# Seven products for a graph layer's weight product, with the sums of the data on GpSimd

## The chip, the cores and the metric

The kernel runs on one core of one Trainium2 chip. The metric is the device time of one execution in microseconds, the median of several. Everything is float32.

The engines are named as the profile names them: PE is TensorE (PEld its loads of the stationary operand), DVE is VectorE, ACT is ScalarE, POOL is GpSimd, SP issues the DMA transfers.

## The reference, cut to what matters

The input `x` has 128 graphs of 64 nodes with 256 features. Four layers follow each other, each with a layer norm and a relu in front and a residual around it: two graph convolutions with LSTMs over windows of nodes, a graph convolution with batch norm, a graph layer with three weights, and causal attention inside each graph. The change concerns the third and touches the operands of the fourth:

```python
h = jnp.maximum(_layernorm(x, axis=-1), 0.0)
adj_0 = jnp.diag(jnp.diagonal(adj)); adj_1 = jnp.triu(adj, k=1); adj_2 = jnp.tril(adj, k=-1)
h = jnp.einsum('bjf,kfo->kbjo', h, W)                  # W: 3 x 256 x 256
out = jnp.einsum('ij,bjo->bio', adj_0, h[0]) + jnp.einsum('ij,bjo->bio', adj_1, h[1]) \
    + jnp.einsum('ij,bjo->bio', adj_2, h[2])
x = x + out + bias
```

## The kernel before, in words

The 8,192 tokens are cut into 16 blocks of 512. The first two layers, with the LSTMs and the two batch norms, take the first 1,460 us; the change leaves their code alone, but the sums of the new weights and the loads of those weights go into the last microseconds of the second layer. Everything else of the change is in the last stage, `rest`, which does layers 3 and 4 for one block.

For a block, `rest` loads the residual `x1` (L1198, a DMA on SP), applies the batch norm of the layer before to the features-by-tokens array (`affine`, L1205, VectorE), turns it to tokens by features on TensorE (`turn`, L1221) and adds `x1` on VectorE (`turned`, L1224). `norm` takes statistics on VectorE (L1235, L1236), the inverse root (`root`: an addition on VectorE, L1240, a power on GpSimd, L1241), the negative mean times that root (`shift`, L1244, VectorE), and normalizes with a relu on ScalarE (L1248). `biased` (L1261) adds the layer's bias to the residual on GpSimd.

`graphs3` (L1273) multiplies by the adjacency's three parts at once: for a half of the features and a half of the tokens, pairs of 64-row matmuls write two PSUM tiles, one copied to `ag` by ScalarE and one by VectorE (L1278). `weigh` (L1285) is the weight product: for each 128 tokens, six matmuls (two halves of the features times three weights) with a piece of `ag` stationary and 256 columns of `wl2` streaming, summed in PSUM. `weighed` (L1291) adds the result to the residual, 512 columns at a time, on VectorE.

Then comes layer 4: the norm again, `h3` turned (L1298) and copied (L1302), and the product with the queries' and keys' joint weights in seven-product form: `qsum` (L1313, VectorE) forms four sums of pieces of the data, `qproduct` (L1326) has seven products that accumulate into three PSUM tiles a, b and c, `qcopy` and `qadd` (L1330, L1333) take these out. `hv` (L1350, copied at L1354) gives the values, `scores` (L1360), `masked` (L1365), `largest` (L1370) and `exps` (L1373) the softmax, `turn_e` (L1381) and `turned_e` (L1385) its transpose, `attend` (L1391) the product with the values, `attended` (L1396, VectorE) adds it to the residual, and a DMA writes the block out (L1402).

The order on each engine is the order in which the program emits instructions. In `rest` every piece of work is put into a list with a label, `at(t, function, ...)`; the list is sorted by the labels and emitted. The labels look like microseconds but set the order alone. Blocks go in pairs, an even one E and an odd one O, with `PERIOD = 52.5` between the labels of two pairs. While a pair's weight products run, the next pair's blocks are turned and normalized (called N here). TensorE's order in a steady pair is: graphs of E and of O, E's products with the transposes of the preceding O's softmax and a turn of N among them, O's products with that O's attend and another turn of N, then E's query product and attention mixed with O's.

[...] `bank()` hands them out in a ring; `new_banks(psum=8)` makes one ring of eight, and a bank is given again only after the last reader of the tile that it held is done.

Of the kernel before, what the change touches and what calls it, by code (L numbers as in the profile page):

```python
# [9 lines left out]
F32 = mybir.dt.float32  # L10
AF = mybir.ActivationFunctionType
ALU = mybir.AluOpType
AX = mybir.AxisListType

P = 128
# [5 lines left out]
def kernel(ctx: ExitStack, tc: tile.TileContext, a: dict, out: bass.AP):  # L21
# [60 lines left out]
    def bank(pool="psum"):  # L82
        return banks[pool][1].tile([P, 512], F32, tag="ps", name="ps")
# [213 lines left out]
    OF = (None, A11, A12, S4, A22, S1, S2, S3)  # L297
# [50 lines left out]
    ROUND, HALF = 10.0, SUP // 2  # L348
# [288 lines left out]
    def at(t, fn, *args):  # L637
        events.append((t, len(events), fn, args))
# [154 lines left out]
    t = 0.0  # L793
    wt[0][0].append(wih0[0])
    for p in range(1, NL + 1):
# [8 lines left out]
        for k in range(0, len(pairs), 2):  # L804
            sts = [{"blk": blk, "N": blk[0][2] * GB, "p": p, "pool": pool}
                   for blk, pool in zip(pairs[k : k + 2], (lh0, lh1))]
            for j in range(p):
                for st in sts:
# [6 lines left out]
                    t = step(t, st, j, j == p - 1, l, wt[l], turn)  # L815
# [82 lines left out]
    with tc.tile_pool(name="pz", bufs=1, reuse_waits="tile") as pz:  # L898
# [13 lines left out]
        B = GATE * (NS - 2)  # L912
# [264 lines left out]

    PERIOD, HALF = 52.5, SUP // 2  # L1180
    NP = NS // 2
    with tc.tile_pool(name="pc", bufs=2, reuse_waits="tile") as pc, \
            tc.tile_pool(name="pc1", bufs=1, reuse_waits="tile") as pc1:
        events = []

        def rest(s, at, only_pair, t_T, t_n, t_G, t_W, t_h, t_QH, t_S, t_soft, t_E, t_O, end):
            first_, v = s == 0, {}
            y = [yslot(s, c) for c in range(KC)]

# [3 lines left out]
            def q2s(k):  # L1193
                return slice(2 * k, 2 * k + 2)
# [31 lines left out]
            def norm(src, tag, halves, t_rows, t_relu):  # L1226

                def new():
                    v["st"] = pc.tile([P, Q, 6], F32, tag="ln_st", name="ln_st", bufs=4)
                    v["mv"] = pc.tile([P, Q, 2], F32, tag="ln_mv", name="ln_mv", bufs=4)  # L1230
                    v["rn"] = pc.tile([P, 2, Q], F32, tag="ln_rn", name="ln_rn", bufs=4)
                    v[tag] = pc.tile([P, Q, D], F32, tag=tag, name=tag)

                def stats(q):
                    nc.vector.bn_stats(v["st"][:, q, :], v[src][:, q, :])  # L1235
                    nc.vector.bn_aggr(v["mv"][:, q, :], v["st"][:, q, :])  # L1236

                def root(qs):
                    rn = v["rn"][:, 0, qs]
                    nc.vector.tensor_scalar_add(rn, v["mv"][:, qs, 1], EPS)  # L1240
                    nc.gpsimd.tensor_tensor(rn, rn, mhalf[:, : qs.stop - qs.start], ALU.pow)  # L1241

                def shift(qs):
                    nc.vector.scalar_tensor_tensor(v["rn"][:, 1, qs], v["mv"][:, qs, 0], -1.0,  # L1244
                                                   v["rn"][:, 0, qs], op0=ALU.mult, op1=ALU.mult)

                def relu(q):
                    nc.scalar.activation(v[tag][:, q, :], v[src][:, q, :], AF.Relu,  # L1248
                                         bias=v["rn"][:, 1, q : q + 1], scale=v["rn"][:, 0, q : q + 1])

                at(t_rows[0] - 0.01, new)
                for q in range(Q):
                    at(t_rows[q // 2] + 0.6 * (q % 2), stats, q)
                for k, qs in enumerate((q2s(0), q2s(1)) if halves else (slice(0, Q),)):
                    at(t_relu[k] - 1.5, root, qs)
                    at(t_relu[k] - 0.1, shift, qs)
# [20 lines left out]
                    to = v["ag"][:, c, :, 2 * k * P : (2 * k + 2) * P]  # L1277
                    copy(to.rearrange("p k (q n) -> p q k n", q=2)[:, :, :, b * T : (b + 1) * T], half[b])  # L1278

            def weigh(k, q):  # L1280
                if q == 0:
                    v["W"] = two(bank())
                for n in range(3 * KC):
                    c, m = divmod(n, 3)
                    nc.tensor.matmul(v["W"][:, q, :], v["ag"][:, c, m, ts(2 * k + q, P)],  # L1285
                                     wl2[m][:, c, :], start=(n == 0), stop=(n == 3 * KC - 1))
# [32 lines left out]
            def qproduct(name, j):  # L1319
                new = ("q", name) not in v  # L1320
                if new:
                    v["q", name] = bank()[:, :HALF]
                if "qk" not in v:
                    v["qk"] = pc1.tile([P, KC, SUP], F32, tag="qk", name="qk")
# [9 lines left out]

            def qdirect(o):
                if o == 0:
                    v["qk"] = pc1.tile([P, KC, SUP], F32, tag="qk", name="qk")
# [65 lines left out]

            at(t_T - 8, load)
            for c in range(KC):
                at(t_T - (2 if first_ else 4.8 if s == 1 else 9) + (0.6 if s != 1 else 0.1) * c, affine, c)
            for k in range(2):
                if first_:
                    at(t_T - (2 - k) * 0.05, turn_chunk, k)
# [2 lines left out]
                at(t_T + 0.1 * k + 0.01, turned, k)  # L1412
            if first_:
                norm("x2", "h2", True, (t_T + 0.455, t_T + 1.8), (t_T + 3.2, t_T + 4.6))
                for q in range(Q):
                    at(t_T + 7 + 0.7 * q, biased, q)
            else:
                norm("x2", "h2", False, (t_n, t_n + 1.2), (t_n + (11.9 if s % 2 and s > 1 else 4.1),))
                for q in range(Q):
                    at(t_n + (18 if s % 2 else 10.5) + 0.7 * q, biased, q)  # L1420
# [47 lines left out]
        for i in range(NP):  # L1468
            t0, first_, end = PERIOD * i, i == 0, i == NP - 1

            def at(t, fn, *args, t0=t0):
                events.append((t0 + t, len(events), fn, args))

            rest(2 * i, at, i, -8.6 if first_ else -40.2, -38.3, 0, (7.0, 12.6), 29.0, 32.6, 40.0, 42.7,
                 46.3 if end else 48.46, 50.4 if end else 50.85, False)
            if first_:
                at(-7.6, weight_product, 2, wo, wvo)
                for k in range(8):
                    at(3.0 + 0.5 * k, qk_weights, k)
            rest(2 * i + 1, at, i, -3.0 if first_ else -27.6, 1.5 if first_ else -25.4, 12.3 if first_ else 3.5, (17.8, 26.5), 39.1,  # L1480
                 (42.0, 45.4, 48.7, 49.6, 52.1) if end else 42.0, 46.7 if end else 48.9,
                 49.5 if end else 59.5, 53.0 if end else 64.7, 53.8 if end else 75.6, end)
        for _, _, fn, args in sorted(events, key=lambda e: e[:2]):
            fn(*args)
    new_banks()
# [38 lines left out]
```

## Time and profile before

| what | us |
|---|---|
| median of 3 runs | 1876.81 (1876.74 to 1877.57) |
| profiled execution, its own time | 1876.78 |
| span of its instructions | 1875.1 |
| PE busy in the span | 1853.9 |
| DVE busy | 1129.4 |
| ACT busy | 925.7 |
| POOL busy | 645.4 |
| last stage, from the first pair's graphs (1461.46) to the end | 413.6 |

The span goes from the first to the last instruction of the profiled execution; 1.7 us of its own time lie around it. Busy time adds up the durations of an engine's instructions, with overlaps counted once. The clock granted to TensorE was 1.00 throughout. In the views, L with a number is a line of the kernel; a group's row gives what it writes and reads, the shapes, the number of instructions after x, then their busy time and the mean of one in ns. Each float32 matmul is two records of TensorE.

### The profile page before, as it was taken

What the parts mean: (1) busy time and instruction counts of PE and PEld (TensorE: products, weight loads), DVE (VectorE), ACT (ScalarE), POOL (GpSimd) and SP (SyncE); (2) the same over time, 40 slices, a digit from 0 to 9 for tenths busy, and PEclk for the clock granted to TensorE, in tenths of its full rate; (3) what the DMA queues carried; (4) which work ended last, traced back from release to release, by engine and by line L of the source; (5) the groups of instructions that cost most, each with busy time, mean ns of one, the idle gap of its engine ahead of it and who ended that gap; (6) DMA issues with size and microseconds to landing.
All of it is one profiled execution on the core that took longest, in us unless ns stands there. A gap on an engine that the chain in (4) does not pass through costs nothing.

```text
span 1875.1 us, 19841 instructions
## 1 busy us (share of the span) xinstructions
PE 1853.9 (99%) x7080; PEld 1168.8 (62%) x7080; DVE 1129.4 (60%) x2254; ACT 925.7 (49%) x1594; POOL 645.4 (34%) x553
## 2 busy tenths in 40 slices
PE   8999999999999999999999999999999999999999
PEld 7997444444445666666444444566444788888887
DVE  6775777634546435445633333588876776667674
ACT  6776666534435334433533333378685434433442
POOL 4451422443424433422442222267353412211220
PEclk9999999999999999999999999999999999999999
DMA  4110001000001000000000000243200111111101
GB/s 146 57 57 1 1 1 29 16 1 0 1 0 45 1 0 1 1 1 1 23 0 0 1 0 0 102 132 116 71 1 2 44 46 46 35 46 46 46 23 34
DMA packets 50642, 54.86 MB, mean 29 GB/s; under 512 B 3184, under 2 KB 45936, under 8 KB 50544
## 3 DMA queue, kind: packets, MB, share of 16 engines
q1 hardware_dynamic: 50096, 53.30, 8.9%
q8 instruction: 56, 0.92, 0.2%
q14 instruction: 42, 0.34, 0.1%
q10 hardware_dynamic: 448, 0.30, 0.0%
HBM read 36.55 MB, written 17.04 MB: 29 GB/s over the span
## 4 chain that ended last, share of the span: by engine, by line
PE 93%; DVE 3%; POOL 1%; ACT 1%; DMA 1%; issue 1%; SPq 0%; ACTq 0%; DVEq 0%; POOLq 0%
PE ps L686 34%; PE ps L692 19%; PE ps L1285 8%; PE ps L930 5%; PE ps L1047 4%; PE ps L1350 3%; PE ps L392 3%; PE ps L402 3%; PE ps L1326 2%; PE ps L431 2%; PE ps L1273 2%; PE ps L1360 2%; PE ps L1391 1%; PE ps L623 1%; PE ps L1298 1%; PE ps L579 1%
## 5 line engine op out<-in xcount | busy, mean ns | idle before, releaser
L708 DVE TENSOR_TENSOR gate<-gate,ps 128x512 f32<-128x512 f32 (+2 forms) x378 | 223.9, 620 | 449.0 <-PE ps L692 367.7
L686 PE MATMUL ps<-tx,wih 128*128 128x512 f32 (+2 forms) x996 | 441.2, 541 | 1.9 <-ACT gate L711 1.0
L686 PE MATMUL ps<-hT,wih 128*128 128x512 f32 (+2 forms) x756 | 338.5, 541 | 0.0
L711 ACT COPY gate<-ps 128x512 f32<-128x512 f32 (+2 forms) x252 | 134.5, 534 | 378.4 <-PE ps L692 325.4
L686 PEld LDWEIGHTS ps<-tx,wih 128*128 128x128 f32 x996 | 188.4, 190 | 188.2 <-issue 128.2
L704 ACT ACTIVATE gate<-gate,lbias 128x512 f32<-128x512 f32 (+2 forms) x252 | 216.7, 860 | 160.0 <-DVE gate L708 160.0
L692 PE MATMUL ps<-h,whh 128*128 128x512 f32 (+2 forms) x576 | 256.6, 527 | 0.0
L686 PEld LDWEIGHTS ps<-hT,wih 128*128 128x128 f32 x756 | 143.6, 190 | 141.6 <-issue 79.4
L692 PE MATMUL ps<-th,whh 128*128 128x512 f32 (+2 forms) x432 | 192.5, 527 | 0.0
L731 POOL TENSOR_TENSOR gate<-gate 128x1024 f32<-128x1024 f32 (+2 forms) x36 | 71.9, 2019 | 297.5 <-ACT gate L704 297.5
L1285 PE MATMUL ps<-wl,ag 128*128 128x256 f32 x768 | 172.1, 380 | 0.0
L692 PEld LDWEIGHTS ps<-h,whh 128*128 128x128 f32 x576 | 109.4, 190 | 100.2 <-issue 76.5
L1285 PEld LDWEIGHTS ps<-wl,ag 128*128 128x128 f32 x768 | 143.4, 190 | 20.2 <-ACT ag L1278 1.8
L731 POOL TENSOR_TENSOR cell<-gate 128x1024 f32<-128x1024 f32 (+2 forms) x36 | 79.4, 2225 | 174.8 <-ACT gate L704 174.8
L1241 POOL TENSOR_TENSOR ln_rn<-ln_rn,mhalf 128x4 f32<-128x4 f32 (+1 forms) x33 | 32.8, 995 | 300.8 <-DVE ln_rn L1240 300.3
L692 PEld LDWEIGHTS ps<-th,whh 128*128 128x128 f32 x432 | 82.1, 190 | 75.2 <-issue 57.4
L1248 ACT ACTIVATE h<-x,ln_rn 128x256 f32<-128x256 f32 x128 | 68.2, 593 | 103.3 <-DVE ln_rn L1244 103.3
L731 POOL TENSOR_TENSOR cell<-gate,cell 128x1024 f32<-128x1024 f32 (+2 forms) x31 | 62.8, 2044 | 110.2 <-ACT gate L704 110.2
L711 DVE COPY gate<-ps 128x512 f32<-128x512 f32 (+2 forms) x126 | 78.6, 624 | 20.8 <-PE ps L692 20.8
L704 ACT ACTIVATE gate<-ps,lbias 128x512 f32<-128x512 f32 (+2 forms) x126 | 79.6, 631 | 3.8 <-PE ps L692 1.0
L736 ACT ACTIVATE gate<-cell 128x1024 f32<-128x1024 f32 (+2 forms) x72 | 68.0, 951 | 26.1 <-POOL cell L731 26.1
L648 DVE TENSOR_TENSOR tx<-hT,tx 128x512 f32<-128x512 f32 (+2 forms) x70 | 57.7, 825 | 13.8 <-PE ps L686 10.2
(236 smaller groups left out, 2933.8 us busy)
## 6 DMA issues: line engine op xcount, KB each, us to landing
xt<-in_x_dram SPq DMA_DIRECT2D x30, 512.0 KB, 4.2
x1d<-xt SPq DMA_DIRECT2D x16, 512.0 KB, 3.0
x<-x1d SPq DMA_DIRECT2D x16, 512.0 KB, 4.9
out_dram<-x SPq DMA_DIRECT2D x15, 512.0 KB, 3.0
wih<-in_WihT_dram SPq DMA_DIRECT2D x16, 256.0 KB, 4.8
whh<-in_WhhT_dram SPq DMA_DIRECT2D x12, 256.0 KB, 4.8
xt<-in_x_dram SPq DMA_DIRECT2D x6, 128.0 KB, 3.2
wl<-in_W_dram SPq DMA_DIRECT2D x3, 256.0 KB, 3.6
```

The source lines that it names most:

```text
L648: yield nc.vector.tensor_sub(t[k], *((b[1][0], b[0][0]), (b[1][1], t[0]), (b[1][1], b[1][0]), (b[0][1], t[1 % len(t)]))[k])
L686: nc.tensor.matmul(wide(p_[:, :N]), wih[0][:, OF[k], gi, :], x_, start=first_, stop=(j == 0), skip_group_check=True)
L692: nc.tensor.matmul(p_[:, :N], whh[0][:, OF[k], gi, :], h_, start=False, stop=True, skip_group_check=True)
L704: nc.scalar.activation(to, r[bank_][:, :N] if bank_ else to, fn, bias=lbias[:, l, m : m + 1])
L708: nc.vector.tensor_add(slot(n, hc), slot(n, hc), r[bank_][:, :N])
L711: op(slot(n, hc), r[bank_][:, :N])
L731: fn(*((t["G"] if isinstance(t, dict) and "G" in t else st["c"])[:, n, :, : st["N"]] for t in tiles))
L736: nc.scalar.activation(o_, c, AF.Tanh)
L930: nc.tensor.matmul(r[name], con["w1"][:, OF[j], g, :], x_, start=new, stop=(name, j) in (("a", 4), ("b", 3), ("c", 2)), skip_group_check=True)
L1047: nc.tensor.matmul(banks[name], w2[:, OF[j], k, :], x_, start=(new and k == 0), stop=(k == 1), skip_group_check=True)
L1248: nc.scalar.activation(v[tag][:, q, :], v[src][:, q, :], AF.Relu, bias=v["rn"][:, 1, q : q + 1], scale=v["rn"][:, 0, q : q + 1])
L1285: nc.tensor.matmul(v["W"][:, q, :], v["ag"][:, c, m, ts(2 * k + q, P)], wl2[m][:, c, :], start=(n == 0), stop=(n == 3 * KC - 1))
```

## The change

The weight product of layer 3 gets the seven-product form that the query product has. `ag`, for each of the three adjacency parts, is cut in 2 x 2 (halves of features by halves of tokens), and so is each weight; four sums of the data (`gsum`, GpSimd, 768 columns each) and four sums of the weights (made once, `weight_sum`, GpSimd) feed seven products in place of eight. Pieces of data and their sums are stationary and 128 columns of weights stream (`gproduct`). The tiles a, b and c that the products accumulate into are taken out, as each partial sum is reached, by four evicts (`gevict`, residual plus tile) and three additions (`gadd`), each of 256 columns on VectorE. Block 0 uses the plain form, with 128 columns streaming too (`gdirect`).

Along with it: the banks become three for these accumulated tiles (`abc`) and a ring of five for all else; `qsum` goes from VectorE to GpSimd; `shift` becomes a multiplication on VectorE in `root` and one on GpSimd; the weights are one tile, loaded by four DMAs; `qk` and the data's sums use the space of weights that are no longer needed. The list is reordered: the next even block is turned at −14.5 where it was at −40.2, the next odd one at −43.5 where it was at −27.6, and the affines, roots, relus and biases that go with them, and O's later steps, get new labels.

```diff
-        wl2 = [weight(f"wl2_{k}", a["W"][k], late) for k in range(3)]
+        wl2 = late.tile([P, 7, 3, P], F32, tag="wl2", name="wl2")
+        for o in range(2):
+            for c in range(2):
+                nc.sync.dma_start(wl2[:, 2 * o + c], a["W"].rearrange(
+                    "m (c p) (o n) -> o c p m n", c=2, o=2)[o, c])
...
+        for k in range(4):
+            if k != 2:
+                at(B + 60 + 5.16 * k, weight_sum, wl2, k)
...
+    new_banks(abc=3, psum=5)
...
                 def root(qs):
-                    rn = v["rn"][:, 0, qs]
+                    rn, nm = v["rn"][:, 0, qs], v["rn"][:, 1, qs]
                     nc.vector.tensor_scalar_add(rn, v["mv"][:, qs, 1], EPS)
+                    nc.vector.tensor_scalar_mul(nm, v["mv"][:, qs, 0], -1.0)
                     nc.gpsimd.tensor_tensor(rn, rn, mhalf[:, : qs.stop - qs.start], ALU.pow)
-
-                def shift(qs):
-                    nc.vector.scalar_tensor_tensor(v["rn"][:, 1, qs], v["mv"][:, qs, 0], -1.0,
-                                                   v["rn"][:, 0, qs], op0=ALU.mult, op1=ALU.mult)
+                    nc.gpsimd.tensor_mul(nm, nm, rn)
...
-            def weigh(k, q):
+            def g_(c, n):
+                return v["ag"][:, c, :, ts(n, HALF)]
+
+            def gsum(k):
+                if k == 0:
+                    v["t2"] = late.tile([P, 3 * KC, D], F32, tag="wT", name="tg")
+                t1, t2 = v["t2"][:, 0:3], v["t2"][:, 3:6]
+                if k == 0:
+                    nc.gpsimd.tensor_sub(t1, g_(0, 1), g_(0, 0))
+                elif k == 1:
+                    nc.gpsimd.tensor_sub(g_(0, 1), g_(1, 1), g_(0, 1))
+                elif k == 2:
+                    nc.gpsimd.tensor_add(t2, g_(0, 1), g_(0, 0))
+                else:
+                    nc.gpsimd.tensor_sub(g_(1, 0), g_(1, 0), t2)
+
+            def gproduct(name, j):
+                new = ("g", name) not in v
+                if new:
+                    v["g", name] = two(bank("abc")[:, :HALF])
+                x_ = (g_(0, 0), g_(1, 0), g_(1, 1), g_(1, 0), v["t2"][:, 0:3] if j == 5 else None,
+                      v["t2"][:, 3:6] if j == 6 else None, g_(0, 1))[j - 1]
+                for p_ in range(2):
+                    for m in range(3):
+                        nc.tensor.matmul(v["g", name][:, p_, :], x_[:, m, ts(p_, P)], wl2[:, OF[j], m, :],
+                                         start=new and p_ == m == 0,
+                                         stop=m == 2 and (name, j) in (("a", 4), ("b", 3), ("c", 2)),
+                                         skip_group_check=True)
+
+            def gdirect(k, q):
                 if q == 0:
                     v["W"] = two(bank())
-                for n in range(3 * KC):
-                    c, m = divmod(n, 3)
-                    nc.tensor.matmul(v["W"][:, q, :], v["ag"][:, c, m, ts(2 * k + q, P)],
-                                     wl2[m][:, c, :], start=(n == 0), stop=(n == 3 * KC - 1))
-
-            def weighed(k):
-                if k == 0:
+                for o in range(KC):
+                    for c in range(KC):
+                        for m in range(3):
+                            nc.tensor.matmul(v["W"][:, q, ts(o, P)], v["ag"][:, c, m, ts(2 * k + q, P)],
+                                             wl2[:, 2 * o + c, m, :], start=(c == 0 and m == 0),
+                                             stop=(c == KC - 1 and m == 2))
...
+            def gevict(o, n, name):
+                if (o, n) == (0, 0):
                     v["x3"] = pc.tile([P, Q, D], F32, tag="x3", name="x3", bufs=4)
-                nc.vector.tensor_add(v["x3"][:, q2s(k)], v["x2"][:, q2s(k)], v["W"])
+                nc.vector.tensor_add(w_("x3", o, n), w_("x2", o, n), v["g", name])
+
+            def gadd(o, n, name):
+                nc.vector.tensor_add(w_("x3", o, n), w_("x3", o, n), v["g", name])
...
-                nc.vector.tensor_sub(t[:, k], *(None, (b_(0, 1), b_(0, 0)), (b_(1, 1), t[:, 1]),
+                nc.gpsimd.tensor_sub(t[:, k], *(None, (b_(0, 1), b_(0, 0)), (b_(1, 1), t[:, 1]),
...
-                    v["q", name] = bank()[:, :HALF]
+                    v["q", name] = bank("abc")[:, :HALF]
...
-                at(t_T - (2 if first_ else 4.8 if s == 1 else 9) + (0.6 if s != 1 else 0.1) * c, affine, c)
+                at(t_T - (2 if first_ else 4.8 if s == 1 else 9 if s % 2 else 16.5) + (0.6 if s != 1 else 0.1) * c, affine, c)
...
-                norm("x2", "h2", False, (t_n, t_n + 1.2), (t_n + (11.9 if s % 2 and s > 1 else 4.1),))
+                norm("x2", "h2", False, (t_n, t_n + 1.2), (t_n + (4.1 if s == 1 else 14.7 if s % 2 else 7.5),))
...
-            for k in range(2):
-                for q in range(2):
-                    at(t_W[k] + 2.6 * q, weigh, k, q)
-                at(t_W[k] + 5.3, weighed, k)
-            norm("x3", "h3", False, (t_W[0] + 5.8, t_W[1] + 5.8), (t_W[1] + 8.8,))
...
+                for t, (name, j) in zip(t_W, (("c", 2), ("a", 1), ("b", 5), ("a", 6), ("b", 3), ("a", 7), ("a", 4))):
+                    at(t, gproduct, name, j)
+                for q in range(Q):
+                    at(t_n + (19.8 if s % 2 and s > 1 else 10.5) + 0.7 * q, biased, q)
+                for t, fn, *args in ((1, gevict, 0, 0, "a"), (2, gevict, 1, 1, "b"), (3, gevict, 0, 1, "a"),
+                                     (6, gevict, 1, 0, "a"), (4, gadd, 0, 1, "b"), (5, gadd, 1, 1, "a")):
+                    at(t_W[t] + 1.35, fn, *args)
+                at(t_W[1] + 1.8, gadd, 0, 0, "c")
+                for k in range(4):
+                    at(t_sums[k], gsum, k)
+            norm("x3", "h3", False, t_Y, (t_relu3,))
...
-            rest(2 * i, at, i, -8.6 if first_ else -40.2, -38.3, 0, (7.0, 12.6), 29.0, 32.6, 40.0, 42.7,
+            rest(2 * i, at, i, -8.6 if first_ else -14.5, -12.5, 0,
+                 (7.0, 9.6, 12.2, 14.8) if first_ else (7.0, 8.3, 9.6, 10.9, 12.2, 13.5, 16.1),
+                 (3.3, 5.2, 7.1, 9.0), (12.5, 17.5) if first_ else (17.9, 15.3), 21.3, 24.6, 31.4, 40.0, 42.7,
...
-            rest(2 * i + 1, at, i, -3.0 if first_ else -27.6, 1.5 if first_ else -25.4, 12.3 if first_ else 3.5, (17.8, 26.5), 39.1,
+            rest(2 * i + 1, at, i, -3.0 if first_ else -43.5, 1.5 if first_ else -41.6,
+                 12.3 if first_ else 3.5, (17.85, 19.6, 20.9, 22.2, 23.5, 24.8, 29.65),
+                 (16.0, 17.0, 18.0, 22.0) if first_ else (12.3, 14.2, 16.1, 22.0), (32.0, 31.2), 35.3, 39.1,
...
```

In the products' names, `("b", 5)` is product 5 added into tile b; the text calls it b5.

More of the change, by code (lines that the diff above doesn't have):

```diff
@@ L1184, with rest @@
         events = []
-        def rest(s, at, only_pair, t_T, t_n, t_G, t_W, t_h, t_QH, t_S, t_soft, t_E, t_O, end):
+        def rest(s, at, only_pair, t_T, t_n, t_G, t_W, t_sums, t_Y, t_relu3, t_h, t_QH, t_S, t_soft, t_E, t_O, end):
             first_, v = s == 0, {}
@@ L1249, in relu @@
                                          bias=v["rn"][:, 1, q : q + 1], scale=v["rn"][:, 0, q : q + 1])
-                at(t_rows[0] - 0.01, new)
+                at(min(t_rows) - 0.01, new)
                 for q in range(Q):
@@ L1255, in norm @@
                     at(t_relu[k] - 1.5, root, qs)
-                    at(t_relu[k] - 0.1, shift, qs)
                     for q in range(qs.start, qs.stop):
@@ L1281, in weigh @@
+            def gdirect(k, q):
                 if q == 0:
                     v["W"] = two(bank())
-                for n in range(3 * KC):
-                    c, m = divmod(n, 3)
-                    nc.tensor.matmul(v["W"][:, q, :], v["ag"][:, c, m, ts(2 * k + q, P)],
-                                     wl2[m][:, c, :], start=(n == 0), stop=(n == 3 * KC - 1))
-            def weighed(k):
-                if k == 0:
+                for o in range(KC):
[4 more added lines that the diff above has]
+                                             stop=(c == KC - 1 and m == 2))
+                if q:
+                    if k == 0:
+                        v["x3"] = pc.tile([P, Q, D], F32, tag="x3", name="x3", bufs=4)
+                    nc.vector.tensor_add(v["x3"][:, q2s(k)], v["x2"][:, q2s(k)], v["W"])
@@ L1290, in weighed, with w_ @@
+            def w_(x, o, n):
+                return v[x][:, q2s(n), ts(o, P)]
+            def gevict(o, n, name):
+                if (o, n) == (0, 0):
                     v["x3"] = pc.tile([P, Q, D], F32, tag="x3", name="x3", bufs=4)
-                nc.vector.tensor_add(v["x3"][:, q2s(k)], v["x2"][:, q2s(k)], v["W"])
+                nc.vector.tensor_add(w_("x3", o, n), w_("x2", o, n), v["g", name])
+            def gadd(o, n, name):
+                nc.vector.tensor_add(w_("x3", o, n), w_("x3", o, n), v["g", name])
@@ L1321, in qproduct @@
                 if new:
-                    v["q", name] = bank()[:, :HALF]
+                    v["q", name] = bank("abc")[:, :HALF]
                 if "qk" not in v:
-                    v["qk"] = pc1.tile([P, KC, SUP], F32, tag="qk", name="qk")
+                    v["qk"] = late.tile([P, KC, 3 * D], F32, tag="wqkv", name="qk")[:, :, :SUP]
                 x_ = (b_(0, 0), b_(1, 0), b_(1, 1), *(v["t"][:, k] for k in (4, 1, 2, 3)))[j - 1]
@@ L1336, in qdirect @@
                 if o == 0:
-                    v["qk"] = pc1.tile([P, KC, SUP], F32, tag="qk", name="qk")
+                    v["qk"] = late.tile([P, KC, 3 * D], F32, tag="wqkv", name="qk")[:, :, :SUP]
                 p_ = bank()
@@ L1414, in rest @@
                 norm("x2", "h2", True, (t_T + 0.455, t_T + 1.8), (t_T + 3.2, t_T + 4.6))
-                for q in range(Q):
-                    at(t_T + 7 + 0.7 * q, biased, q)
-            else:
-                norm("x2", "h2", False, (t_n, t_n + 1.2), (t_n + (11.9 if s % 2 and s > 1 else 4.1),))
-                for q in range(Q):
-                    at(t_n + (18 if s % 2 else 10.5) + 0.7 * q, biased, q)
+            else:
+                norm("x2", "h2", False, (t_n, t_n + 1.2), (t_n + (4.1 if s == 1 else 14.7 if s % 2 else 7.5),))
             for k in range(4):
                 at(t_G + 0.8 * k, graphs3, *((k % 2, k // 2) if first_ else (k // 2, k % 2)))
-            for k in range(2):
-                for q in range(2):
-                    at(t_W[k] + 2.6 * q, weigh, k, q)
-                at(t_W[k] + 5.3, weighed, k)
-            norm("x3", "h3", False, (t_W[0] + 5.8, t_W[1] + 5.8), (t_W[1] + 8.8,))
+            if first_:
+                for k in range(4):
+                    at(t_W[k], gdirect, k // 2, k % 2)
+                    at(t_T + 7 + 0.7 * k, biased, k)
+            else:
+                for t, (name, j) in zip(t_W, (("c", 2), ("a", 1), ("b", 5), ("a", 6), ("b", 3), ("a", 7), ("a", 4))):
[6 more added lines that the diff above has]
+                at(t_W[1] + 1.8, gadd, 0, 0, "c")
+                for k in range(4):
+                    at(t_sums[k], gsum, k)
+            norm("x3", "h3", False, t_Y, (t_relu3,))
             for c in range(KC):
@@ L1477 @@
                 at(-7.6, weight_product, 2, wo, wvo)
+                at(17.0, weight_sum, wl2, 2)
                 for k in range(8):
-                    at(3.0 + 0.5 * k, qk_weights, k)
-            rest(2 * i + 1, at, i, -3.0 if first_ else -27.6, 1.5 if first_ else -25.4, 12.3 if first_ else 3.5, (17.8, 26.5), 39.1,
+                    at(4 + 0.5 * k, qk_weights, k)
+            rest(2 * i + 1, at, i, -3.0 if first_ else -43.5, 1.5 if first_ else -41.6,
+                 12.3 if first_ else 3.5, (17.85, 19.6, 20.9, 22.2, 23.5, 24.8, 29.65),
+                 (16.0, 17.0, 18.0, 22.0) if first_ else (12.3, 14.2, 16.1, 22.0), (32.0, 31.2), 35.3, 39.1,
                  (42.0, 45.4, 48.7, 49.6, 52.1) if end else 42.0, 46.7 if end else 48.9,
-                 49.5 if end else 59.5, 53.0 if end else 64.7, 53.8 if end else 75.6, end)
+                 49.5 if end else 59.5, 53.0 if end else 67.35, 53.8 if end else 79.5, end)
         for _, _, fn, args in sorted(events, key=lambda e: e[:2]):
```

## The prediction

> **What bounds the kernel now.** I read four views: the page, the stretches cut at the start of each pair of blocks, the chain that ended last inside one pair, and the grouped instructions of five pairs with the shapes kept apart. First the page's head.
>
> ```profile
> span 1875.1 us, 19841 instructions
> PE 1853.9 (99%) x7080; PEld 1168.8 (62%) x7080; DVE 1129.4 (60%) x2254; ACT 925.7 (49%) x1594; POOL 645.4 (34%) x553
> ```
>
> The change touches only the last stage, eight pairs from 1461.46 to the end. In the stretches (length, then PE, PEld, DVE, ACT, POOL busy) the first, a steady and the last pair read:
>
> ```profile
> 1461.46:1512.79 51.33, 50.37 (x297) 43.22 (x297) 37.70 (x98) 22.86 (x52) 19.42 (x30) 1.00 0.04 11
> 1563.67:1614.55 50.88, 50.88 (x309) 45.45 (x308) 36.58 (x95) 20.23 (x52) 10.09 (x12) 1.00 0.13 42
> 1818.09:1875.07 56.98, 52.49 (x299) 44.58 (x298) 28.60 (x71) 17.61 (x50) 2.03 (x2) 1.00 0.11 37
> ```
>
> A steady pair is TensorE alone; GpSimd works 10.1 of 50.9 us. From start to start of its records TensorE waits only 0.4 us in such a pair (0.2 of it before the turns of h3), 2.1 in the first. The chain inside the pair (start, us, what) gives the pace:
>
> ```profile
> 1569.14 5.38 PE ps L1285 x24
> 1574.52 0.44 PE ps L1381 x4
> 1574.96 0.87 PE ps L1221 x8
> 1575.83 10.36 PE ps L1285 x48
> ...
> 1602.41 1.79 PE ps L1360 x16
> ```
>
> A record is half a float32 matmul. 48 of 256 columns take 10.36 us, 0.216 each; 16 of 128 columns take 1.79, 0.112 each, a little more than half. A pair's weight product is 96 records: 20.74 us.
>
> [...] The trace agrees on the lock; its timeline (start, us):
>
> ```profile
> 1292.70 0.17 DVE L607 TENSOR_SCALAR ln_rn<-ln_mv 128x4 f32<-128x4 f32 x1
> 1300.73 1.27 POOL L835 TENSOR_TENSOR T<-ag 128x512 f32<-128x512 f32 x1 [4.04 <-PE ps L930]
> 1301.39 0.64 DVE L607 TENSOR_SCALAR ln_rn<-ln_mv 128x4 f32<-128x4 f32 x1
> ```
>
> The same four columns take 0.17 alone, but behind a GpSimd sum ending at 2.00 they end at 2.03. DVE work fed from PSUM, and statistics, show no such wait. The rows that I price with:
>
> ```profile
> L1285 PE MATMUL ps<-wl,ag 128*128 128x256 f32 x480 | 107.4, 380 | 0.0
> L1261 POOL TENSOR_TENSOR x<-x,bl 128x256 f32<-128x256 f32 x40 | 30.3, 784 | 7.4 <-ACT h L1248 7.4
> L1241 POOL TENSOR_TENSOR ln_rn<-ln_rn,mhalf 128x4 f32<-128x4 f32 x20 | 20.3, 1014 | 196.6 <-DVE ln_rn L1240 196.6
> L1278 DVE COPY ag<-ps 128x384 f32<-128x384 f32 x40 | 20.4, 553 | 4.4 <-PE ps L1273 4.4
> L1396 DVE SCALAR_TENSOR_TENSOR x<-ps,mx,x 128x256 f32<-128x256 f32 x41 | 17.6, 471 | 0.9 <-PE ps L1391 0.9
> L1205 DVE TENSOR_SCALAR hT<-hT,co 128x512 f32<-128x512 f32 x20 | 10.6, 528 | 0.0
> ```
>
> **The change, part by part.**
>
> *Matmuls.* 15 of 16 blocks go from 48 records of 256 columns (10.37 us) to 7 products x 6 matmuls x 2 = 84 records of 128 (x 0.1117 = 9.38): −0.985 us a block, −1.97 a pair. Block 0 stays direct but streams 128 columns: 96 x 0.1117 = 10.72, +0.35. All: −14.4.
>
> *Sums on GpSimd.* No trace row has 768 columns; 512 take 1.27 and 1024 take 2.35, so 1.8 (ends 1.5 and 2.1). Eight a pair are 14.4. Eight moved qsums at 0.73, eight biased rows at 0.78, four pow at 1.01 and four multiplies at 0.2 (by L610's 201 ns) give about 31 of 51 us: not a bound by its sum, but by order it can be late.
>
> *VectorE.* A block's two 512-column adds (0.68) become seven of 256 columns at 0.415 (L1333's row): +1.5 a block. The qsums leave (−2.4), four shifts become four tensor_scalars of 0.17. It goes to 38 of 51 us: free unless order delays it.
>
> *Loads.* Four loads of the layer's weights replace three, and x1's are issued at other places, each landing in 3.5 to 6.4 us; by the new list the margins stay over 1 us: nothing. If one is late, it is late once, by about 1.
>
> *Banks.* Three PSUM banks go to the seven-form products; the rest share five in a ring instead of eight. In the built program the graphs' fourth step (L1273 before) now waits for the preceding even block's second attended to free its bank. On VectorE that stands behind the copy of the first step and behind one affine, moved there. From the start of graphs: copy 0.99 to 1.47, affine 0.46, attended 0.87, so it ends at 2.8; the odd block's first step then needs a VectorE copy ending at 3.7. Walked through, graphs take 6.3 to 6.45 instead of 5.40 us: about +1.0. Behind these matmuls stands all of TensorE's list.
>
> *Even block's products.* Product a6 needs the first evict, which stands behind two turned adds: +0.2. The last, a4, needs the add into b: +0.3.
>
> *Odd block's products.* With X the end of E's last product, gsum 3 of O starts on GpSimd at X+3.4 [...]. The first affine of the next even block is due at X+3.6 on VectorE and waits until 5.2; two affines end at 6.1, the evict of b behind them at 6.5, and b3 needs its bank. It was due at X+5.36: +1.1, with the restart up to +1.3. VectorE's later evicts, the root and the relus behind them move along, but meet slack. If the affine comes first, gsum waits and the two alternate: +1.45. The unknown is the lock for this operation: it never overlapped GpSimd before. Bounds 0 to 1.5; I take 1.25, since [...] L607, a tensor_scalar too, shows the wait.
>
> *What is won besides.* The turn of the next even block now stands before O's h3, and its 0.2 stall goes.
>
> Steady pair: 50.88 − 0.4 (old waits) − 1.97 + 0.1 (waits that stay) = 48.6, and + 1.05 + 0.2 + 0.3 + 1.25 = 2.8 gives 51.4: **+0.56, six times +3.4**. Between 51.0 and 51.7 the terms' ends leave +0.1 to +0.8.
>
> *First pair.* 51.33 − 2.1 (old waits) − 0.98 + 0.35 + 0.1 = 48.7. New waits: the direct product behind a copy that an affine holds up, 1.2; the weights' third sum and two gsums in a row before a6, 0.9 to 1.4; the root's tensor_scalars and an affine blocked by gsums before b3, up to 2.3. Some overlap, so +1.0 to +2.6 on 51.33; I take +1.8. *Last pair.* No affine, no next block: −1.97 with some 0.8 of waits, −1.2.
>
> Sum: 3.4 + 1.8 − 1.2 = +4.0. On the profiled execution's 1876.78 (span 1875.1 plus 1.7 around it, 0.03 under the median of three) that is 1880.8.
>
> **The rivals.** (The bound between same and different is 0.2%, 3.75 us, about what a measurement of this kernel can tell from no change.)
>
> *B, the saving lands whole.* The 99% speaks for it: a list bound by TensorE where every new wait hides. 1876.8 − 14.4 = 1862.4. Against it: attended stands behind copy and affine in the built order.
>
> *C, the lock does not reach the affine* (the other side). Place: O's b3, beside gsum 3; price 1.25 in each of six pairs and about 1.6 of the first: 9.1. Without it 1880.8 − 9.1 = 1871.7. It decides from where the lock costs below about 0.2 a pair (faster by 0.2%); below 0.7 the kernel breaks even. For it: the affine was never seen beside GpSimd, and GpSimd need only start 0.4 us later for the affine to pass. Against it: L607.
>
> *D, the lock bites but the ring of banks does not*: attended frees its bank early enough. Less 0.9 x 6: 1875.4, the same. For it: in the kernel before attended follows the first copy at once and nothing on TensorE waited for it. Against it: there were eight banks, and no affine between.
>
> *E, GpSimd gets late*: its blocked and blocking sums of O push a6 and a7 too, as its order is strict: root, qsums and biased wait in one queue. Another 1 us in seven pairs: 1888. For it: two thirds busy with single waits up to 1.8. Against it: TensorE meets the sums only at b5, a6, a7 and a4.
>
> **How the numbers follow.** Forecast A, +2 to +6: 0.40, of which 0.15 lies within 0.2%. B 0.10, C 0.17, D 0.15, E 0.18. Faster B + C = 0.27; same 0.15 + 0.15 = 0.30; slower 0.25 + 0.18 = 0.43. A's own range is 1878.8 to 1882.8. The range must reach C below (and with bank waits half as long, 0.5 x 7 less, 1868) and E above (1888), and leaves out B and E's tail, together under 0.2.
>
> **What would show it.** Records of the products 0.112 apart; steady pairs near 51.4 with about 2.8 us of TensorE waits: 1.0 in graphs, released by attended and a VectorE copy; 1.2 before O's b3, with an affine of 1.5 us or more beside a gsum. Affines of 0.5 there mean C; graphs of 5.4 mean D. GpSimd near 31 us a pair; much over it means E. It goes wrong if 128-column records with changing loads pace slower than 0.112 (each 0.01 is +12 in all), or if waits in a row fold into one.

## The result, and the profile after

The changed kernel takes 1881.51 us (median of 11 runs, 1881.01 to 1881.94) where the kernel before took 1876.74 beside it: a ratio of 1.0025, 95% interval 1.0015 to 1.0034. It is slower, by 4.8 us (0.25%); 1880.8 had been forecast. The profiled execution's span is 1879.3 where it was 1875.1. In what follows a line number is that of the changed kernel unless the kernel before is named: graphs are L1278 with copies at L1283, the products L1311, the affine L1213, evicts and additions L1336 and L1339, attended L1444, the fourth data sum L1301.

The page's head and the stretches (length, then PE, PEld, DVE, ACT, POOL busy), cut again where each pair's graphs begin:

```profile
span 1879.3 us, 21335 instructions
PE 1851.2 (99%) x7668; PEld 1181.0 (63%) x7668; DVE 1123.7 (60%) x2269; ACT 924.9 (49%) x1594; POOL 805.2 (43%) x710
```

```profile
1460.75:1513.68 52.93, 50.88 (x380) 46.24 (x380) 34.32 (x94) 23.13 (x52) 34.68 (x49) 1.00 0.04 11
1616.88:1668.53 51.65, 50.49 (x381) 46.47 (x381) 35.99 (x97) 20.11 (x52) 30.57 (x32) 1.00 0.13 42
1823.46:1879.30 55.84, 51.27 (x371) 45.47 (x370) 30.11 (x77) 17.61 (x50) 19.72 (x16) 1.00 0.12 39
```

TensorE still reads 99%: the share hides the change altogether. The lengths show it. The first pair grew from 51.33 to 52.93, a steady pair from 50.88 to 51.64, the last fell from 56.98 to 55.84: +1.6, +4.5 for six pairs (one of them is 51.57) and −1.1. The stage also begins 0.7 us earlier, as it does by 0.1 to 1.0 in every variant of the changed kernel below; why stays open. Together +4.2, the difference of the spans.

The chain that ended last, in one steady pair (start, us, what), is no longer TensorE alone:

```profile
1616.96 0.90 PE ps L1278 x8
...
1617.95 0.56 DVE ag L1283
1618.51 0.46 DVE hT L1213
1618.96 0.79 DVE x L1444 x2
1619.76 0.04 issue
1619.80 0.92 PE ps L1278 x8
...
1632.97 0.02 issue
1632.99 0.43 DVE x L1339
...
1637.86 0.43 DVE x L1336
1638.29 0.02 issue
1638.31 0.42 DVE x L1339
1638.73 2.16 DVE hT L1213 x2
1640.89 0.34 DVE x L1336
1641.23 0.04 issue
1641.27 1.61 PE ps L1311 x12
```

At the top the graphs wait for attended, which stands on VectorE behind the first copy and one affine. In the middle a4, which adds into tile a, waits for the addition on VectorE that takes a7's sum out of that tile. At the bottom b3 of the odd block, which adds into tile b, waits for the evict of b, and that stands behind two affines which take 2.16 us. The timeline there (start, us) shows whom the affines wait for:

```profile
1638.33 1.82 POOL L1301 TENSOR_TENSOR ag<-ag,tg 128x768 f32<-128x768 f32 x1
1638.65 2.24 DVE L1213 TENSOR_SCALAR hT<-hT,co 128x512 f32<-128x512 f32 x2
1640.81 0.74 DVE L1336 TENSOR_TENSOR x<-x,ps 128x256 f32<-128x256 f32 x2
```

Of a pair's four affines (least, median and greatest ns in the row below) three take 0.54 us, and the one that starts beside the sum 1.79: it ends 0.3 after the sum does.

```profile
L1213 DVE TENSOR_SCALAR hT<-hT,co x4: 534/539/1786, 1618.4 to 1640.4; 128x512 f32<-128x512 f32 x4
```

From start to start of its records, TensorE's waits in a steady pair are 1.23 in the graphs (6.63 in place of 5.40), 0.19 before a6, 0.33 before a4 and 0.94 before b3, and after most of these waits the next record comes 0.07 to 0.1 late as well.

### The profile page after: what moved, and what is told of

It is laid out like the page before. It is cut to its first block, busy times and chain, and to the rows that moved or that the text cites. A ratio compares the mean times of both kernels' runs of the same rounds, so it can differ in the third digit from the quotient of the medians.

```text
span 1879.3 us, 21335 instructions
## 1 busy us (share of the span) xinstructions
PE 1851.2 (99%) x7668; PEld 1181.0 (63%) x7668; DVE 1123.7 (60%) x2269; ACT 924.9 (49%) x1594; POOL 805.2 (43%) x710
## 4 chain that ended last, share of the span: by engine, by line
PE 91%; DVE 5%; POOL 1%; ACT 1%; issue 1%; DMA 1%; SPq 0%; DVEq 0%; POOLq 0%; ACTq 0%
PE ps L686 34%; PE ps L692 19%; PE ps L1311 7%; PE ps L930 5%; PE ps L1047 4%; PE ps L1398 3%; PE ps L392 3%; PE ps L402 3%; PE ps L1374 2%; PE ps L431 2%; PE ps L1278 2%; PE ps L1408 2%; PE ps L1439 1%; PE ps L623 1%; DVE hT L1213 1%
## 5 line engine op out<-in xcount | busy, mean ns | idle before, releaser
L1254 ACT ACTIVATE h<-x,ln_rn 128x256 f32<-128x256 f32 x128 | 68.1, 591 | 114.8 <-POOL ln_rn L1251 114.8
L1311 PE MATMUL ps<-wl,ag 128*128 128x128 f32 x900 | 109.9, 278 | 6.4 <-DVE x L1336 4.6
L1311 PEld LDWEIGHTS ps<-wl,ag 128*128 128x128 f32 x900 | 104.6, 192 | 11.1 <-DVE x L1336 5.8
L648 DVE TENSOR_TENSOR tx<-hT,tx 128x512 f32<-128x512 f32 (+2 forms) x70 | 57.7, 824 | 13.9 <-PE ps L686 10.3
L731 POOL TENSOR_TENSOR cell<-cell,gate 128x1024 f32<-128x1024 f32 (+2 forms) x31 | 65.5, 2133 | 0.4
```

The source lines that it names most:

```text
L648: yield nc.vector.tensor_sub(t[k], *((b[1][0], b[0][0]), (b[1][1], t[0]), (b[1][1], b[1][0]), (b[0][1], t[1 % len(t)]))[k])
L731: fn(*((t["G"] if isinstance(t, dict) and "G" in t else st["c"])[:, n, :, : st["N"]] for t in tiles))
L1311: nc.tensor.matmul(v["g", name][:, p_, :], x_[:, m, ts(p_, P)], wl2[:, OF[j], m, :], start=new and p_ == m == 0, stop=m == 2 and (name, j) ...
```

## The experiments

Two theories are to be parted from each other and from rivals: that graphs wait for banks that attended frees (ring theory; a bank is one of the kernel's eight PSUM tiles of 512 float32 columns), and that an affine blocked by a GpSimd sum holds up b3 (lock theory). All pair lengths are read from the start of the graphs' first matmul to that of the next pair; graphs, from that start to the first product. Each ratio is to the kernel before run beside that variant. Its medians lie between 1876.4 and 1877.0, so times of different rows can be compared to about 0.6 us. A steady pair's length is the one that most pairs of a run share; in e11 the first two are longer, 50.14 and 50.00.

| run | time, us | ratio to before (95%) | steady pair | graphs |
|---|---|---|---|---|
| before | 1876.4 to 1877.0 | | 50.88 | 5.40 |
| after | 1881.51 | 1.0025 (1.0015 to 1.0034) | 51.64 | 6.63 |
| e1, even affines later | 1875.38 | 0.9991 (0.9984 to 0.9997) | 50.60 | 6.63 |
| e2, fourth sum later | 1875.43 | 0.9990 (0.9981 to 0.9998) | 50.60 | 6.63 |
| e3, odd affines earlier | 1877.24 | 1.0000 (0.9991 to 1.0009) | 50.91 | 5.90 |
| e4, one ring of banks | 1874.39 | 0.9986 (0.9979 to 0.9992) | 50.80 | 5.79 |
| e5, before with the split | 1880.76 | 1.0023 (1.0014 to 1.0031) | 51.31 | 5.84 |
| e6, both affines moved | 1871.81 | 0.9974 (0.9964 to 0.9984) | 50.03 | 5.90 |
| e8, and one ring | 1866.11 | 0.9943 (0.9928 to 0.9958) | 49.53 | 5.40 |
| e9, and the odd turn moved | 1869.62 | 0.9962 (0.9947 to 0.9977) | 50.04 | 5.40 |
| e10, and its statistics later | 1861.57 | 0.9919 (0.9904 to 0.9933) | 48.87 | 5.40 |
| e11, e8 with qsums on VectorE | 1868.61 | 0.9956 (0.9939 to 0.9972) | 49.82 | 5.40 |

**The lock.** e1 takes the affines away from the sum:

```diff
-                at(t_T - (2 if first_ else 4.8 if s == 1 else 9 if s % 2 else 16.5) + (0.6 if s != 1 else 0.1) * c, affine, c)
+                at(t_T - (2 if first_ else 4.8 if s == 1 else 9 if s % 2 else 2) + (0.6 if s != 1 else 0.1) * c, affine, c)
```

> The changed kernel with one edit: the two affines of the next even block stand 14.5 labels later, behind the query product's last additions, where VectorE and GpSimd are both idle in the trace. Lock theory (the affines wait for the fourth data sum of O and hold up the evict of b): the 1.0 us wait before O's b3 goes, a steady pair falls from 51.64 to about 50.6, the time from 1881.5 to about 1874. Rival one, that the affines' own 0.92 us of VectorE work and no lock holds up the evict: the same here, so this run tells both from rival two. Rival two, that b3 waits for something else than VectorE's order (the data's sums or matmul pace): 51.6, 1881.5.

The pair fell to 50.60, the wait before b3 is gone, and the other waits of a steady pair stand. But both the lock and the affines' own time left with that edit. e2 leaves the affines where they are and moves the sum:

```diff
-                 (16.0, 17.0, 18.0, 22.0) if first_ else (12.3, 14.2, 16.1, 22.0), (32.0, 31.2), 35.3, 39.1,
+                 (16.0, 17.0, 18.0, 24.5) if first_ else (12.3, 14.2, 16.1, 24.5), (32.0, 31.2), 35.3, 39.1,
```

> The changed kernel with one edit: the fourth data sum of odd blocks gets label 24.5 where it had 22.0, so that GpSimd makes it behind the next odd block's power and not beside the affines, which stay where they are. Lock theory: the affines take 0.5 us each, the evict of b follows 1.3 us earlier, the wait before O's b3 goes, pair about 50.6 and time about 1874, as in the run with the affines moved. Rival one (the affines' own work, no lock): nothing changes before b3, pair 51.6. If the sum is now too late for a4, a new wait before a4 shows instead.

The pair is 50.60 again. VectorE's timeline and GpSimd's in that run:

```profile
1636.53 0.42 DVE L1339 TENSOR_TENSOR x<-x,ps 128x256 f32<-128x256 f32 x1
1636.87 1.00 DVE L1213 TENSOR_SCALAR hT<-hT,co 128x512 f32<-128x512 f32 x2
1637.79 0.41 DVE L1336 TENSOR_TENSOR x<-x,ps 128x256 f32<-128x256 f32 x1
```

```profile
1636.40 0.20 POOL L1251 TENSOR_TENSOR ln_rn<-ln_rn 128x4 f32<-128x4 f32 x1
1639.34 1.01 POOL L1250 TENSOR_TENSOR ln_rn<-ln_rn,mhalf 128x4 f32<-128x4 f32 x1 [2.74 <-DVE ln_rn L1249]
```

GpSimd is idle from 1636.60 to 1639.34, and the same two affines in the same place take 1.00 us together, not 2.24. VectorE still does their work ahead of the evict, and b3 doesn't wait. So it is the overlap that cost 1.04 us a pair, not the affines' place in the queue. The rival of own work is out.

**The ring.** e3 takes the affine out of the graphs, e4 undoes the split of the banks, and e5 puts the split alone into the kernel before:

```diff
-                at(t_T - (2 if first_ else 4.8 if s == 1 else 9 if s % 2 else 16.5) + (0.6 if s != 1 else 0.1) * c, affine, c)
+                at(t_T - (2 if first_ else 4.8 if s == 1 else 9 if s == 3 else 25.3 if s % 2 else 16.5) + (0.6 if s != 1 else 0.1) * c, affine, c)
```

> The changed kernel with one edit: the two affines of the next odd block leave the graphs and stand 16 labels earlier, in the idle time of VectorE at the end of the pair before. Ring theory (the graphs wait for attended, and it stands behind copy and affine): attended ends 0.46 us earlier and the second copy 0.9 earlier, the graphs take about 5.8 us in place of 6.6, pair about 50.8, time about 1876. Rival (the graphs wait for the copies' data or for the relu, not for banks that attended frees): graphs 6.6, pair 51.6, 1881.5.

```diff
-    new_banks(abc=3, psum=5)
+    new_banks(psum=8)
...
-                    v["g", name] = two(bank("abc")[:, :HALF])
+                    v["g", name] = two(bank()[:, :HALF])
...
-                    v["q", name] = bank("abc")[:, :HALF]
+                    v["q", name] = bank()[:, :HALF]
```

> The changed kernel with the split of the banks alone undone: one ring of eight banks for everything, the accumulated tiles among them. Ring theory: no bank of the graphs waits for attended or for the second copy any more, whatever stands before them on VectorE: graphs about 5.5, pair about 50.5, time about 1874, unless the long-lived accumulated tiles bring a new wait in the ring. Rival (VectorE's order holds the graphs up through their data, not through banks): 51.6, 1881.5.

```diff
+    new_banks(abc=3, psum=5)
     PERIOD, HALF = 52.5, SUP // 2
...
-                    v["q", name] = bank()[:, :HALF]
+                    v["q", name] = bank("abc")[:, :HALF]
```

> The kernel before with the change's split of the banks alone: three for the query product's accumulated tiles, five for all else. Ring theory: the graphs' fourth step now waits for attended here too, but with no affine between the first copy and attended it ends at about 2.3 us after the graphs' start, the step is due at 2.0 and the next step waits less: graphs 5.7 to 5.9 in place of 5.4, pair 51.2 to 51.4, time about 1880. Rival (the split is harmless and the affine in the graphs alone makes the wait): pair 50.88, time 1876.9.

e3 won 0.73 (0.9 expected: graphs 5.90, not 5.8), e4 0.84 with the affine still in place (1.05 to 1.1 expected: graphs 5.79, not 5.5; the waits left come in the seventh of the eight steps, presumably because a bank of it is read late, and they are gone in e8, which has the affine out too). e5 lost 0.43 a pair without any affine there, as the ring theory had it; its chain shows the graphs alone stretched. The first line is e4's, the others e5's:

```profile
1664.39 5.79 PE ps L1278 x64
1614.84 1.29 PE ps L1392 x6
1616.13 5.83 PE ps L1274 x62
1621.97 2.14 PE ps L1286 x9
```

The split of the banks, a line of the change that computes nothing, by itself costs the kernel before 4.4 us (1880.76 against 1876.40). In e4 the first pair also fell, from 52.94 to 50.95, so 2.0 us of that pair were the ring's.

**Do the gains add?** e6 has the edits of e1 and e3, e8 that of e4 besides.

```diff
-                at(t_T - (2 if first_ else 4.8 if s == 1 else 9 if s % 2 else 16.5) + (0.6 if s != 1 else 0.1) * c, affine, c)
+                at(t_T - (2 if first_ else 4.8 if s == 1 else 9 if s == 3 else 25.3 if s % 2 else 2) + (0.6 if s != 1 else 0.1) * c, affine, c)
```

> The changed kernel with both affines moved to the idle end of the pair (the next even block's and the next odd block's). If the two waits are independent, their gains add: pair 51.64 - 1.04 - 0.73 = 49.87, time about 1871. Rival (the four affines in a row there delay the turn or the copies of h3, or the wait gained in the graphs is met again later): pair 50.3 or more, time 1873.5 or more.

> The changed kernel with both affines moved and with one ring of eight banks. Graphs back to 5.4, no wait before O's b3, the first pair about 51: pair about 49.3 (51.64 - 1.04 - 1.23), time about 1866, which is 1862.4 with the waits before a6 and a4 (0.5 a pair) left. Rival (with eight banks in one ring the accumulated tiles, held over many steps, bring waits of their own once the others are gone): pair 49.8 or more, time 1870 or more.

They add, nearly: 50.03 where 49.87 was expected, 49.53 where 49.3 was. In e8 the waits left are those before a6 (0.19) and a4 (0.33), and 0.11 inside the next even block's turn, which now comes on the heels of its affines; that one, with 0.06 on the record after it, is in e6 also and makes up the 0.16 missing in both. e9 goes for the first two: the next odd block's turn stands between a7 and a4, and its load, affines, relu and bias keep their absolute labels.

```diff
-            at(t_T - 8, load)
+            at(t_T - (14.6 if s % 2 and s > 1 else 8), load)
...
-                at(t_T - (2 if first_ else 4.8 if s == 1 else 9 if s == 3 else 25.3 if s % 2 else 2) + (0.6 if s != 1 else 0.1) * c, affine, c)
+                at(t_T - (2 if first_ else 4.8 if s == 1 else 15.6 if s == 3 else 31.9 if s % 2 else 2) + (0.6 if s != 1 else 0.1) * c, affine, c)
...
-                norm("x2", "h2", False, (t_n, t_n + 1.2), (t_n + (4.1 if s == 1 else 14.7 if s % 2 else 7.5),))
+                norm("x2", "h2", False, (t_n, t_n + 1.2), (t_n + (4.1 if s == 1 else 8.1 if s % 2 else 7.5),))
...
-                    at(t_n + (19.8 if s % 2 and s > 1 else 10.5) + 0.7 * q, biased, q)
+                    at(t_n + (13.2 if s % 2 and s > 1 else 10.5) + 0.7 * q, biased, q)
...
-            rest(2 * i + 1, at, i, -3.0 if first_ else -43.5, 1.5 if first_ else -41.6,
+            rest(2 * i + 1, at, i, -3.0 if first_ else -36.9, 1.5 if first_ else -35.0,
```

> As the run with one ring and both affines moved, and the next odd block's turn also stands between E's a7 and a4 where it stood between a1 and b5. The two waits left in E's products should go: a6 no longer finds turned ahead of the evict of a, and a4 has 0.87 us more of TensorE work between it and a7. Pair about 48.8, time about 1863. Rival (turned and the statistics, later by 6 us, now come between the additions of E and make a4, the root or h3 late): pair 49.3 or more, time 1866 or more.

The rival won by its size, though not at the place it named. Both waits went, and a new one of 1.1 us came, not in E's products but before O's a6; the pair is 50.04. The chain there:

```profile
1677.61 1.26 DVE x L1232 x2
1678.87 0.35 DVE ln_st L1243
...
1682.84 0.13 DVE ln_rn L1248
1682.98 0.07 DVE ln_rn L1249
1683.05 0.33 DVE x L1336
1683.38 0.14 issue
1683.52 2.92 PE ps L1311 x24
```

The evict of O's first tile (1683.05) stands behind five microseconds of turned adds and of two blocks' statistics. So e10 leaves the turn there and moves what nobody waits for, the odd block's statistics, root, relu and bias, needed only in the next pair's graphs:

```diff
-                norm("x2", "h2", False, (t_n, t_n + 1.2), (t_n + (4.1 if s == 1 else 8.1 if s % 2 else 7.5),))
+                norm("x2", "h2", False, (t_n, t_n + 1.2), (t_n + (4.1 if s == 1 else 13.5 if s % 2 else 7.5),))
...
-                    at(t_n + (13.2 if s % 2 and s > 1 else 10.5) + 0.7 * q, biased, q)
+                    at(t_n + (18.0 if s % 2 and s > 1 else 10.5) + 0.7 * q, biased, q)
...
-            rest(2 * i + 1, at, i, -3.0 if first_ else -36.9, 1.5 if first_ else -35.0,
+            rest(2 * i + 1, at, i, -3.0 if first_ else -36.9, 1.5 if first_ else -27.5,
```

> As the run with the turn between a7 and a4, but the next odd block's statistics stand 7.5 labels later and its root and relu 12.9 later, behind O's first evicts. There the statistics of two blocks in a row had held up O's evict of a and made a wait of 1.1 us before O's a6. If that queue was the cause, the wait goes and pairs fall from 50.04 to about 49.0, the time to about 1863. Rival (VectorE has too much to do in O's products wherever the statistics stand): pair 49.5 or more, time 1866 or more.

The pair is 48.87, with nothing but TensorE on its chain; the kernel takes 1861.57 us in all, 0.8% under the kernel before and 1.1% under the changed one with the same arithmetic. The first view is one pair's stretch, the second a part of the chain in the next pair.

```profile
1608.75:1657.62 48.87, 48.87 (x383) 45.97 (x382) 35.17 (x97) 20.16 (x52) 30.58 (x32) 1.00 0.14 44
```

```profile
1663.08 8.23 PE ps L1311 x72
1671.32 0.44 PE ps L1429 x4
1671.76 0.87 PE ps L1229 x8
1672.63 8.04 PE ps L1311 x72
1680.67 0.87 PE ps L1346 x8
```

**Was the move of the query's sums to GpSimd free?** e11 is e8 with them back on VectorE:

```diff
-                nc.gpsimd.tensor_sub(t[:, k], ...
+                nc.vector.tensor_sub(t[:, k], ...
```

> As the run with one ring and both affines moved, with the query sums back on VectorE. If VectorE has room for them and GpSimd was not what anything waited for, as the prediction costed them: pair 49.5, time 1866, the same. Rival one, GpSimd was late in places: faster by some tenths a pair. Rival two, VectorE is late with the sums behind its statistics, or its sums of two SBUF operands meet GpSimd's biased: slower by 0.3 or more a pair, 1868.5 or more.

Slower than e8 by 0.29 a pair, and by about 2 us in all when each is set against the kernel before that ran beside it (8.3 us under it here, 10.3 in e8). That is nearest to rival two. Two rows of its pair:

```profile
L1346 PEld LDWEIGHTS ps<-ident,h 128*128 128x128 f32 x16 | 1.8, 141 | 0.2 <-ACT h L1254 0.2
L1361 DVE TENSOR_TENSOR tq<-h3T,tq 128x256 f32<-128x256 f32 x4 | 2.3, 580 | 0.0
```

TensorE now waits 0.17 in the turn of h3, for a relu (L1254) whose root is late, and 0.10 before the scores; e8 has neither wait. In that pair four of the eight sums start beside GpSimd's `biased` and take 0.57 to 0.94 us; the other four take 0.39 to 0.42. So the overlap costs VectorE about 1.5 us of the pair. How much of the 0.29 comes of that and how much of the sums' own place in VectorE's queue, this run doesn't tell. The kernel before paid it too: of the four sums of one block there (from 1552.33), three took 0.83 to 0.94 beside `biased`, and one 0.41. In e8's arrangement the move to GpSimd is a gain, not nothing.

## Why the prediction was right

**Matmuls.** −1.97 a pair was forecast from 0.1117 us a record. e10, with the waits out, shows 72 records in 8.04 us, 0.1117 each, and a pair 2.01 under that of before. The saving is whole; in the changed kernel waits cover it. The pace came out as forecast because it was read from the scores (L1360 of the kernel before), which have one load for each record as the products have (32 and 32 in a pair, 168 and 168 of the products). The records of the loads at L1311 last 192 ns on average, longer than that pace, and overlap.

**Graphs.** Forecast +1.05 by way of attended behind copy and affine; measured +1.23, by that way: the chain has copy, affine and attended in a row, attended ends 2.87 us after the graphs began, where 2.8 had been worked out, and the fourth step goes on at 2.92. Split and affine make each other worse: graphs of 5.40 become 5.79 with the affine alone (e4), 5.90 with the split alone (e6), 6.63 with both. The e5 run shows the split's part, 0.43 a pair, without the rest of the change.

**Odd block's b3.** Forecast +1.25 with the restart, measured 0.94 and 0.1. An affine takes 1.79 us beside the sum and 0.54 without it: with 1.50 of the sum left when it started, it waited out that whole remainder. In the trace of before no affine started beside a GpSimd sum; that it would wait as L607 had was my estimate. e2 shows the overlap as the cause; what the two meet at, no run shows. The wait goes both ways: in the trace of before the 21 `biased` additions that started inside a query sum took 0.82 to 0.91 us, the other 43 took 0.72 to 0.74. It isn't every operation of VectorE: `weighed` (L1291 there), which reads PSUM, took 0.69 us beside `biased` and 0.66 to 0.69 without, and statistics (L602) 0.39 to 0.42 beside GpSimd's sums and without. Nor is it every GpSimd instruction: in the first pair an affine that started inside a GpSimd power (1485.27) took 0.53.

**Even block's a6 and a4.** 0.2 and 0.3 forecast, 0.19 and 0.33 measured, 0.26 and 0.40 with the late record after each. What a4 waits for is the addition that reads tile a after a7; if "the add into b" meant the one that reads tile b, the place was wrong and the size right.

**The sum.** Pair 51.44 forecast, 51.64 measured; +3.4 for six pairs became +4.5. That the pair is within 0.2 is in part luck: the graphs' term came out 0.18 over its forecast and b3's 0.21 under, and the two cancel. What is left is small: a6 and a4 with their late records (+0.16), and old waits of which about 0.2 a pair went where a net 0.3 had been taken off. First pair 53.1 forecast (+1.8), 52.93 measured (+1.6); last −1.2 and −1.1.

**GpSimd.** A sum of 768 columns takes 1.81 us (1.8 taken from the two neighbouring widths), and a pair 30.57 (31). None of TensorE's waits in the steady pair is put down to it. Rival E is out, but for one wait of 0.8 before a4 in the first pair.

**What failed.** The first pair's size was right and its parts were not: I had put up to 2.3 of its waits on the root and an affine blocked by sums, and 1.2 on a copy behind an affine. One ring alone took 2.0 out of it (e4), while e1 and e2 moved it by 0.2 or less: it was mostly banks, and the size agreed by luck. VectorE was to come to 38 us a pair; it came to 36, with 1.25 of that the affine's wait. The terms of the prediction, +1.5 and −2.4 a block, give 34.8; the total was added wrongly, and no term rested on it. A pace slower by 0.01 would have cost 13.6 us over 1,356 records, not 12. And moving the query's sums was given no price for TensorE: e11 puts 0.3 a pair on it once the rest is tight.

**The rivals.** B's 1862.4, the saving without any wait, was the right price for another order of the list and other banks: e10 reaches 1861.57. C is refuted by the 1.79 us affine and e2, D by e4 and e5.

## What to carry to other kernels

When a kernel is bound by one engine, an edit that shortens that engine's work is worth only what the orders of the other engines let through: price each new wait from the built order, by what stands ahead of the releaser in its queue. Splitting a ring of buffers is such an edit even when nothing in the arithmetic changes, and a VectorE operation of the kinds seen to wait here, a scaling or a sum from SBUF to SBUF, should be costed with the rest of a GpSimd sum that it starts beside (0.54 us became 1.79 for an affine, 0.39 became 0.94 for a query sum). When a wait is removed by moving work, look at what the moved work now stands in front of; here work with a whole pair of slack was what could be moved out of the way.

## What the runs showed that was not expected

Three banks taken out of a ring of eight cost 0.43 us a pair in the kernel before (e5), though its graphs had no wait and the accumulated tiles went to banks of their own; conversely one ring of eight with tiles held over seven products brought no wait to the graphs in e8 and e10. And between the changed kernel and e10, the same matmuls, sums and evicts in another order and with other banks differ by 20 us, of a stage of 419 in the changed kernel.
